# Two graph products by Strassen's scheme: three of their seven half-size products split once more

## The chip, the cores and the metric

The kernel runs on one core of one Trainium2 chip. The metric is the device time of one execution in microseconds (us). The runs of the kernel before took 618.68, 618.24 and 617.34; their median is 618.24.

## The reference

The inputs are x of shape (16, 1024, 64), that is 16 graphs ("batches") of 1024 nodes with 64 channels, and one matrix adj of 1024 x 1024. Everything is float32. Layer 0 is an attention whose scores are multiplied with adj, layer 1 a diffusion convolution with the same adj in both places; each is added to its input and normalised over the 64 channels.

```python
# layer 0
Q, K, V = x @ Wq.T + bq, x @ Wk.T + bk, x @ Wv.T
score = softmax(einsum('bnc,bmc->bnm', Q, K), axis=1)
score = einsum('bnm,mc->bnc', score, adj)
x = layernorm(x + einsum('bnm,bmc->bnc', score, V))
# layer 1, with support0 = support1 = adj
x1 = einsum('ij,bjk->bik', adj, x0)
x2 = 2 * einsum('ij,bjk->bik', adj, x1) - x0
# both supports start from x0, so the second gives the same x1 and x2
out = concatenate([x0, x1, x2, x1, x2], -1) @ weight + bias
x = layernorm(x0 + out)
```

Since both supports are adj, layer 1 with the residual comes down to x0 Wa + adj (x0 Wb) + adj (adj (x0 Wc)) with three folded 64x64 weights. The kernel computes it as two products with adj, one inside the other: Z = x0 Wb + adj (x0 Wc), and then x0 Wa + bias + adj Z. In layer 0, adj V is computed as adj x, since the value weight can be applied later. So the kernel has three products of a 1024x1024 matrix with a 1024x1024 matrix (1024 nodes by 16 batches of 64 channels).

## The kernel before

The 16 batches are worked on as 8 pairs, so a pair fills 128 columns; the 1024 nodes are 8 blocks of 128. `xs` holds x by pairs and blocks, `xT` its transposed form, `GY` the rows of x0 Wc (and, at the end, the output), `aT` the transposed adj.

**The products.** `product` computes one 1024x1024 product by Strassen's scheme in Winograd's form: seven products p1 to p7 of 512x512 quarters. The left factors are quarters of adj or the sums S1 to S4 (`left_sum`, lines 216 to 222; S3 overwrites a quarter of `aT`), the right factors are quarters of the other matrix or the sums T1 to T4 (`sums`, lines 247 to 253). Each sum is one VectorE instruction of 128 x 2048. One `step(name, g)` issues half of one of the seven products: two block rows of the result, each four matmuls of 128x512 into one PSUM bank (line 284), and then one read of the 128x1024 PSUM tile by VectorE or ScalarE (lines 300 to 304), which adds it to the place of the result. Chains of products add up in PSUM: p1, p6, p7 and p4 run on in one tile ("a"), p5 and p3 in another ("b"), p2 alone ("c"), and between two members of a chain the partial sum is read and added to another quarter of the result. So a sum that belongs to two quarters is made once.

**Order of the work.** The tiles are under a manual schedule: each engine executes its instructions in the order of the program text, and the framework adds the semaphore waits, for single tile regions. The stages are: loads, transposes and projections (to 29 us in the profile), the first product adj x (to about 125 us), the attention in 64 steps (8 pairs x 8 blocks, to 410 us), the second product (to about 502 us) and the third (to 609 us). In the attention, each step issues the scores of the step after next (line 323), the running minimum on VectorE (line 330), the exponentials on ScalarE (line 337) and the weighted sums (line 360). When a pair is done, `take`, `norm_1`, `norm_2`, `transposed` and `weigh` normalise it, transpose it and apply the folded weights, spread over the steps of the next pair. `weigh` (lines 396 to 410) leaves x0 Wc in `GY`, x0 Wa + bias in `xT` and x0 Wb in `xs`. For the last pair all this falls into the first part of the second product, between its matmuls.

The second product starts with p2 and writes its result to `Z`, which takes over the memory of `U` (the result of the first, adj x); its first read of each quarter adds x0 Wb from `xs`. The third starts from x0 Wa + bias in `xT` and writes to `GY`. `leave` (line 525 on) normalises what is finished: square on ScalarE, row sum on VectorE (line 192 or 179), the inverse root either on GpSimd (line 185) or on ScalarE and VectorE (lines 194 and 195), the scaling (line 531) on GpSimd or VectorE, and the output DMA from the SP queue. The end of the third product is cut into block rows, so that four such chains follow one another.

[...] the kernel uses them as three tiles `ps` and one tile `acc` of two banks each.

Of the kernel before, what the change touches and what calls it, by code (L numbers as in the profile page):

```python
# [9 lines left out]
FP = mybir.dt.float32  # L10
# [8 lines left out]
def gnn_kernel(  # L19
# [85 lines left out]
    def transposed(p):  # L105

        pt = ps_tile("pt")
        for k in range(K8):
            nc.tensor.transpose(pt[:, ts(k, P)], xs[:, p, k, :], ident)  # L109
        nc.scalar.activation(xT[:, p], pt, AF.Copy)  # L110
# [89 lines left out]

    att = ctx.enter_context(tc.tile_pool(name="att", bufs=1))
# [11 lines left out]

    def left_sum(S, n):
        if n == 1:
            nc.vector.tensor_add(S[1], aT[:, low, right], aT[:, high, right])
        elif n == 2:
            nc.vector.tensor_sub(S[2], S[1], aT[:, low, left])
        elif n == 3:
            nc.vector.tensor_sub(aT[:, low, right], aT[:, low, left], aT[:, low, right])  # L220
        else:
            nc.vector.tensor_sub(S[4], aT[:, high, left], S[2])

    def by_pair(t):

        return t.rearrange("p k (q f) -> p q k f", q=NP)

    def product(S, src, res, plus=None, acc_group=0):

        pairs, blocks = (slice(0, NP // 2), slice(NP // 2, NP)), (low, high)
        T, open_, seen = {}, {}, set()

        def src_q(j, c):
            return src[:, pairs[c], blocks[j]]

        def by_pair4(t):
            return t.rearrange("p k (q f) -> p q k f", q=NP // 2)  # L240

        def sums(n):
            if n == 1:
                T[1] = quarter_tile("r", "T", 1)
            t = by_pair4(S[1] if n == 3 else T[1])
            if n == 1:
                nc.vector.tensor_sub(t, src_q(0, 1), src_q(0, 0))
            elif n == 2:
                nc.vector.tensor_sub(t, src_q(1, 1), t)
            elif n == 3:  # L250
                nc.vector.tensor_sub(t, src_q(1, 1), src_q(0, 1))
            else:
                nc.vector.tensor_sub(t, src_q(1, 0), t)  # L253

        def quarter(j, c):
            return lambda k: src[:, pairs[c], j * HB + k]

        def of(t):
            return lambda k: t()[:, k]


        table = {
            "p2": (lambda k, i: aT[:, HB + k, ts(i, P)], quarter(1, 0), "c", (0, 0)),
            "p1": (lambda k, i: aT[:, k, ts(i, P)], quarter(0, 0), "a", (0, 0)),
            "p5": (lambda k, i: S[1][:, k, ts(i, P)], of(lambda: T[1]), "b", (1, 1)),
            "p3": (lambda k, i: S[4][:, k, ts(i, P)], quarter(1, 1), "b", (0, 1)),
            "p6": (lambda k, i: S[2][:, k, ts(i, P)], of(lambda: T[1]), "a", (0, 1)),
            "p7": (lambda k, i: aT[:, k, ts(HB + i, P)], of(lambda: S[1]), "a", (1, 1)),
            "p4": (lambda k, i: aT[:, HB + k, ts(HB + i, P)], of(lambda: T[1]), "a", (1, 0)),
        }  # L270
        first_of = {"p2": True, "p1": True, "p5": True}

        def step(name, g, rows=(0, 1)):
            left_of, right_of, chain, (qi, qc) = table[name]
            start = name in first_of
            if start and rows[0] == 0:
                if chain == "a" and g == acc_group:
                    open_[chain, g] = pacc.tile([P, N], FP, tag="acc", name="acc")
                else:
                    open_[chain, g] = ps_tile(name)  # L280
            pt = open_[chain, g]
            for i in rows:
                for k in range(HB):
                    nc.tensor.matmul(  # L284
                        pt[:, ts(i, H)], left_of(k, 2 * g + i), right_of(k),
                        start=(start and k == 0), stop=(k == HB - 1), skip_group_check=not start,
                    )
            got = pt.rearrange("p (i q f) -> p q i f", i=2, q=NP // 2)[
                :, :, rows[0] : rows[-1] + 1
            ]  # L290
            b0 = qi * HB + 2 * g + rows[0]

            def at(t):
                return t[:, pairs[qc], b0 : b0 + len(rows)]

            mark = (qi, qc, g, rows[0]) if len(rows) == 1 else (qi, qc, g)
            known = any(m in seen for m in (mark, mark[:3]))
            seen.add(mark)
            if known:
                nc.vector.tensor_add(at(res), got, at(res))  # L300
            elif plus is None:
                nc.scalar.activation(at(res), got, AF.Copy)  # L302
            else:
                nc.vector.tensor_add(at(res), got, at(plus))  # L304

        return step, sums
# [64 lines left out]
    def norm_1(p):  # L371
        po = ps_tile("po")
# [17 lines left out]
    def weigh(p, c):  # L390

        pw = ps_tile("pw").rearrange("p (b f) -> p b f", b=2)
# [10 lines left out]
        def at(t):  # L403
# [7 lines left out]
            xs[:, p, blocks].rearrange("p k (b c) -> p k b c", b=2), to[:, 1], AF.Copy  # L411
        )

    S = left_tiles()
    for n in (1, 2, 4, 3):
        left_sum(S, n)
    step, sums = product(S, xs, by_pair(U), acc_group=1)
    sums(1)
# [4 lines left out]
    for name in ("p2", "p1", "p5"):  # L423
        step(name, 0)
        step(name, 1)
    sums(2)
    sums(3)
    step("p3", 0)
    step("p6", 0)
    step("p6", 1)  # L430
    sums(4)
    step("p7", 0)
    step("p7", 1)
    step("p3", 1)
    step("p4", 0)
    for i in range(2):
        step("p4", 1, (i,))
        scores(i)
        for j in range(2):
            exponentials(i, j)  # L440
# [6 lines left out]

    last = len(steps) - 1
    for n, (p, m) in enumerate(steps):
        if n + 2 <= last:  # L450
            scores(n + 2)
            exponentials(n + 2, 0)
# [18 lines left out]

    def blocked(t):
        return t.rearrange("p q (k f) -> p q k f", k=K8)

    p = NP - 1
    Z = big.tile([P, K8, BC], FP, tag="uz", name="Z")
    root = const.tile([P, 1], FP, tag="root", name="root")
    nc.scalar.activation(root, eps, AF.Sqrt)
    S = left_tiles()
    step, sums = product(S, blocked(GY), by_pair(Z), xs)  # L480
    weigh(p - 1, 3)
    step("p2", 0, (0,))
    norm_1(p)
    norm_2(p, last=True)
    step("p2", 0, (1,))
    left_sum(S, 1)
    step("p2", 1)
    transposed(p)
    step("p1", 0, (0,))
    weigh(p, 0)  # L490
    weigh(p, 1)
    step("p1", 0, (1,))
    weigh(p, 2)
    weigh(p, 3)
    sums(1)
    step("p1", 1)
    left_sum(S, 2)
    left_sum(S, 4)
    step("p5", 0)
    left_sum(S, 3)  # L500
    step("p5", 1)
    sums(2)
    sums(3)
    step("p3", 0)
    step("p6", 0)
    step("p6", 1)
    sums(4)
    step("p7", 0)
    step("p7", 1)
    nc.vector.tensor_add(S[1], S[2], aT[:, low, left])  # L510
    step("p4", 0)
    step("p4", 1)
    step("p3", 1)

    R = GY.rearrange("p q n -> p (q n)").rearrange("p (k f) -> p k f", k=K8)

    def leave(i, c, g, skip=0, blocks=2):

        first_block = i * HB + 2 * g + skip
        r = R[:, first_block : first_block + blocks, ts(c, H)].rearrange(  # L520
            "p i (b c) -> p i b c", c=C
        )
        nb = B // 2
        sq = att.tile([P, blocks, nb, C], FP, tag="rT", name="sq2")
        nc.scalar.activation(sq, r, AF.Square)  # L525
        rows = sq.rearrange("p i b c -> p (i b) c")
        if blocks == 1:
            engine, rstd = nc.vector, inverse_root_2(rows, nb)
        else:
            engine, rstd = nc.gpsimd, inverse_root(row_sums(rows))  # L530
        engine.tensor_tensor(  # L531
            r, r, rstd.rearrange("p (i b) c -> p i b c", i=blocks), ALU.mult
        )
        for n in range(blocks):
            nc.sync.dma_start(out[ts(first_block + n, P), ts(c, nb)], r[:, n])

    step, sums = product(S, by_pair(Z), by_pair(R), blocked(xT))
    step("p2", 0)
    sums(1)
    step("p2", 1)  # L540
    for g in range(2):
        step("p1", g)
        leave(0, 0, g)
    step("p5", 0)
    step("p5", 1)
    sums(2)
    sums(3)
    step("p3", 0)
    step("p6", 0)
    leave(0, 1, 0)  # L550
    step("p6", 1)
    sums(4)
    for g in range(2):
        step("p7", g)
        leave(1, 1, g)
    step("p4", 0)
    leave(1, 0, 0)
    for i in range(2):
        for name, q in (("p4", (1, 0)), ("p3", (0, 1))):
            step(name, 1, (i,))  # L560
            leave(*q, 1, i, 1)
# [40 lines left out]
```

## Time and profile before

| | before |
|---|---|
| median of the runs | 618.24 us |
| the profiled execution, its own time | 617.97 us |
| its span | 616.0 us |
| busy: TensorE / VectorE / ScalarE / GpSimd | 605.6 / 337.1 / 226.0 / 78.4 us |
| TensorE busy in the second and third product (410 to 609 us) | 198.9 of 199.0 us |
| VectorE busy there | 81.9 us |
| mean granted TensorE clock | 0.997 of full speed |
| longest row of waits that ended TensorE's idle time | 1.5 us in all, for the first transposes |

The profile shows one execution. Lines of the form "start, length, engine, line, operation, out<-in, shape" are instructions in order of time; what stands in brackets is the idle time before an instruction and what ended it. A float32 matmul shows as two records, each with its own weight load (PEld). The length of a VectorE instruction reaches to the moment its result is written; the next one may start some 0.08 us before that.

### The profile page before, as it was taken

The page shows a single profiled execution, that of the slowest core. Times are in us where ns is not written, and L with a number is a line of the kernel's source. Part 1 is how long each engine was busy: PE and PEld are TensorE (multiplying, and loading weights), DVE is VectorE, ACT ScalarE, POOL GpSimd, SP SyncE. Part 2 cuts the span into 40 slices and gives each one's busy share as a digit, 9 for nine tenths or more (in the row PEclk, how much of TensorE's full clock was granted, in tenths as well). Part 3 has the DMA queues.
Part 4 walks back from the last instruction along what each step waited for, and adds up shares of the span by engine and source line. Part 5 has one row for each costly group of instructions (what it writes and reads, how often), then busy time and mean ns, then how long its engine had stood idle before and what let it go on. Part 6 is the DMA issues. An engine that isn't in the chain of part 4 may idle for free. (4 is left out here: it accounts for less than half of the span.)

```text
span 616.0 us, 5816 instructions
## 1 busy us (share of the span) xinstructions
PE 605.6 (98%) x2270; PEld 264.4 (43%) x2270; DVE 337.1 (55%) x560; ACT 226.0 (37%) x379; POOL 78.4 (13%) x40
## 2 busy tenths in 40 slices
PE   8999999999999999999999999999999999999995
PEld 7544444433334344443434434344444444444442
DVE  1696212067677767677776767735462333224535
ACT  4210110156666666676666667651100000000012
POOL 0000004400030300203030020300000000150372
PEclk9999999999999999999999999999999999999998
DMA  8700000000000000000000000000000000010012
GB/s 302 263 0 1 0 1 36 33 0 1 1 1 0 2 1 1 1 1 1 1 0 2 0 2 1 0 1 0 1 0 1 0 0 0 1 69 0 34 70 102
DMA packets 6763, 14.30 MB, mean 23 GB/s; under 512 B 2000, under 2 KB 2000, under 8 KB 6736
## 3 DMA queue, kind: packets, MB, share of 16 engines
q1 hardware_dynamic: 6416, 13.90, 6.1%
q8 instruction: 18, 0.29, 0.2%
q10 hardware_dynamic: 320, 0.03, 0.0%
q14 instruction: 9, 0.07, 0.0%
HBM read 9.73 MB, written 4.19 MB: 23 GB/s over the span
## 5 line engine op out<-in xcount | busy, mean ns | idle before, releaser
L330 DVE TENSOR_SCALAR_CACHE_REDUCE e<-sc 128x1024 f32<-128x1024 f32 x128 | 151.6, 1222 | 68.1 <-PE sc L323 68.1
L337 ACT ACTIVATE e<-e,nm 128x1024 f32<-128x1024 f32 x128 | 146.2, 1143 | 74.6 <-DVE e L330 74.5
L323 PE MATMUL sc<-xT,GY 64*128 64x512 f32 x512 | 128.1, 615 | 0.5 <-DVE e L330 0.5
L360 PE MATMUL acc<-e,us 128*64 128x512 f32 x512 | 124.0, 605 | 0.3 <-DVE us L348 0.3
L185 POOL TENSOR_TENSOR rstd<-var,expo 128x16 f32<-128x16 f32 x13 | 37.7, 2901 | 421.5 <-DVE var L180 421.5
L323 PEld LDWEIGHTS sc<-xT,GY 64*128 64x128 f32 x512 | 44.6, 186 | 73.5 <-issue 49.9
L525 ACT ACTIVATE sq<-GY 128x1024 f32<-128x1024 f32 (+1 forms) x10 | 8.9, 886 | 159.6 <-DVE GY L300 149.9
L284 PE MATMUL p<-T,S 128*128 128x512 f32 x144 | 62.8, 592 | 0.0
L360 PEld LDWEIGHTS acc<-e,us 128*64 128x64 f32 x512 | 31.0, 136 | 71.0 <-issue 62.9
L284 PEld LDWEIGHTS p<-T,S 128*128 128x128 f32 x144 | 27.4, 190 | 34.4 <-issue 34.4
L302 ACT ACTIVATE U<-p 128x1024 f32<-128x1024 f32 x6 | 6.1, 1024 | 76.3 <-PE p L284 76.3
L396 PEld LDWEIGHTS pw<-raw,xT 64*128 64x128 f32 x256 | 21.8, 187 | 17.3 <-issue 7.3
L444 POOL TENSOR_TENSOR xs<-xs,mu 128x1024 f32<-128x1024 f32 x8 | 15.0, 1901 | 102.8 <-DVE T L253 92.0
L396 PE MATMUL pw<-raw,xT 64*128 64x192 f32 x256 | 27.1, 332 | 0.0
L407 DVE TENSOR_TENSOR xT<-pw,raw 128x256 f32<-128x256 f32 x32 | 13.6, 425 | 21.3 <-ACT GY L406 21.3
L337 ACT ACTIVATION_READ_ACCUMULATOR e<-e,nm 128x1 f32 x128 | 24.0, 188 | 0.0
L110 ACT ACTIVATE xT<-pt 128x1024 f32<-128x1024 f32 x16 | 16.2, 1014 | 17.2 <-PE pt L109 17.2
L284 PE MATMUL acc<-T,aT 128*128 128x512 f32 x48 | 21.4, 594 | 0.0
L284 PE MATMUL p<-GY,aT 128*128 128x512 f32 x48 | 21.3, 596 | 0.0
L284 PE MATMUL p<-T,aT 128*128 128x512 f32 x48 | 21.3, 592 | 0.0
L284 PE MATMUL acc<-T,S 128*128 128x512 f32 x48 | 21.1, 592 | 0.0
L284 PE MATMUL p<-S,aT 128*128 128x512 f32 x48 | 21.1, 592 | 0.0
(116 smaller groups left out, 585.4 us busy)
## 6 DMA issues: line engine op xcount, KB each, us to landing
aT<-in_adjT_dram SPq DMA_DIRECT2D x8, 512.0 KB, 11.3
out_dram<-GY SPq DMA_DIRECT2D x16, 256.0 KB, 2.2
xs<-in_x_dram SPq DMA_DIRECT2D x7, 512.0 KB, 6.4
aT<-in_adjT_dram SPq DMA_DIRECT2D x1, 1024.0 KB, 5.2
xs<-in_x_dram SPq DMA_DIRECT2D x2, 256.0 KB, 3.0
w1s<-in_w_dram SPq DMA_DIRECT2D x2, 80.0 KB, 10.0
wq<-in_wqT_dram ACTq DMA_DIRECT2D x2, 16.0 KB, 3.3
wk<-in_wkT_dram SPq DMA_DIRECT2D x2, 16.0 KB, 3.1
```

Source lines behind the costliest of these rows:

```text
L110: nc.scalar.activation(xT[:, p], pt, AF.Copy)
L185: nc.gpsimd.tensor_tensor(rstd, var, expo[:, 0:g], ALU.pow)
L284: nc.tensor.matmul(pt[:, ts(i, H)], left_of(k, 2 * g + i), right_of(k), start=(start and k == 0), stop=(k == HB - 1), skip_group_check=not ...
L302: nc.scalar.activation(at(res), got, AF.Copy)
L323: nc.tensor.matmul(sc[j][:, ts(h, H)], GY[s, p, ts(m, P)], xT[s, p, ts(h, H)], start=True, stop=True,)
L330: nc.vector.tensor_scalar(E[n][:, j], sc[j], -1.0, None, op0=ALU.mult, op1=ALU.min, accum_out=NM[n][:, j : j + 1],)
L337: nc.scalar.activation(E[n][:, j], E[n][:, j], AF.Exp, bias=NM[n][:, j : j + 1], scale=-1.0, accum_out=SM[n][:, j : j + 1],)
L360: nc.tensor.matmul(ACC[p][j * C : (j + 1) * C, ts(h, H)], us[:, j], es[:, j, ts(h, H)], start=(m == 0), stop=(m == K8 - 1),)
L396: nc.tensor.matmul(pw[:, j, ts(k, 3 * C)], xT[s, p, ts(2 * c + k, P)], raw[s, 0:3].rearrange("p w c -> p (w c)"), start=True, stop=True,)
L407: nc.vector.tensor_tensor(at(xT), to[:, 0], raw[:, 4:5, None].to_broadcast([P, 2, 2, C]), ALU.add)
L444: nc.gpsimd.tensor_tensor(rows_of(p), rows_of(p), mu[:, p, :, None].to_broadcast([P, G, C]), ALU.subtract)
L525: nc.scalar.activation(sq, r, AF.Square)
```

## The change

The second and third product are issued by a new class `Product`. It differs from `product` in these points.

- Every left and right sum is four instructions of 128 x 512 (one for each block of rows) instead of one of 128 x 2048. This holds for the first product as well.
- A list `line` holds pieces of VectorE work that wait to be issued. `later` appends to it, `fill(n)` issues the next n, `need(names)` issues from it until no piece of these names is left. `step` issues its matmuls, then its reads, then `fill(fills)`.
- In the second and third product the half-size products 2, 3 and 4 are each split again by the same scheme: `halves` gives the eight sums of 256x256 quarters (each one VectorE instruction of 128 x 512, kept in the memory of `xs`), and `part` issues one of the seven small products, four matmuls of 128x256 into one bank and one VectorE read of 128 x 512. Parts 1, 6, 7 and 4 share one bank, 5 and 3 another, 2 has its own.
- Products 3 and 4 no longer add up in the PSUM chains; so the PSUM tiles of 5 and of 7 are read into two quarters each (`twice`).
- `weigh` leaves x0 Wb in `U`, the place of adj x, a pair at a time after that pair's attention; the second product adds to it there, and the third reads it. `Z` is gone.
- The second product starts with product 1 and the tile of the attention's accumulator; the order is 1, 2, 5, 3, 6, 7, 4 in both. The first eight small sums are issued in the last eight steps of the attention.
- `leave` works on two blocks by four or eight batches; its first instruction, the square, is issued at once and the rest is put at the head of `line`.

The diff, cut to its core:

```diff
     def left_sum(S, n):
-        if n == 1:
-            nc.vector.tensor_add(S[1], aT[:, low, right], aT[:, high, right])
-        elif n == 2:
-            nc.vector.tensor_sub(S[2], S[1], aT[:, low, left])
-        elif n == 3:
-            nc.vector.tensor_sub(aT[:, low, right], aT[:, low, left], aT[:, low, right])
-        else:
-            nc.vector.tensor_sub(S[4], aT[:, high, left], S[2])
+        to, a, b, op = {
+            1: (S[1], aT[:, low, right], aT[:, high, right], ALU.add),
+            2: (S[2], S[1], aT[:, low, left], ALU.subtract),
+            3: (aT[:, low, right], aT[:, low, left], aT[:, low, right], ALU.subtract),
+            4: (S[4], aT[:, high, left], S[2], ALU.subtract),
+        }[n]
+        return [
+            lambda k=k: nc.vector.tensor_tensor(to[:, k], a[:, k], b[:, k], op)
+            for k in range(HB)
+        ]
...
+    line = []
+    def later(name, pieces):
+        line.extend((name, piece) for piece in pieces)
+    def fill(n):
+        for _ in range(min(n, len(line))):
+            line.pop(0)[1]()
+    def need(*names):
+        while any(name in names for name, _ in line):
+            fill(1)
...
+        def targets(self, name):
+            return {
+                1: [(0, 0)], 2: [(0, 0)], 3: [(0, 1)], 4: [(1, 0)], 6: [(0, 1)],
+                5: [(1, 1)] + [(0, 1)] * (3 in self.twice),
+                7: [(1, 1)] + [(1, 0)] * (4 in self.twice),
+            }[name]
...
+        def step(self, name, g, fills=0, rows=(0, 1)):
+            self.matmuls(name, g, rows)
+            self.read(name, g, rows)
+            fill(fills)
...
+        def halves(self, name, room):
+            a, b = self.factors(name)
+            W = H // 2
+            la = [[a[:, 2 * j : 2 * j + 2, ts(i, W)] for j in range(2)] for i in range(2)]
+            rb = [[b[:, 2 * c : 2 * c + 2, 2 * j : 2 * j + 2] for c in range(2)] for j in range(2)]
+            s, t, raw_t = {}, {}, {}
+            for n in range(1, 5):
+                s[n] = room[:, ts(n - 1, H)].rearrange("p (k i) -> p k i", k=2)
+                t[n] = by_pair(room[:, ts(n + 3, H)].rearrange("p (k f) -> p k f", k=2))
+            self.sub = {
+                1: (la[0][0], rb[0][0]), 2: (la[0][1], rb[1][0]), 3: (s[4], rb[1][1]),
+                4: (la[1][1], t[4]), 5: (s[1], t[1]), 6: (s[2], t[2]), 7: (s[3], t[3]),
+            }
+            sub, add = nc.vector.tensor_sub, nc.vector.tensor_add
+            lefts = [
+                lambda: add(s[1], la[1][0], la[1][1]), lambda: sub(s[2], s[1], la[0][0]),
+                lambda: sub(s[3], la[0][0], la[1][0]), lambda: sub(s[4], la[0][1], s[2]),
             ]
+            rights = [
+                lambda: sub(t[1], rb[0][1], rb[0][0]), lambda: sub(t[2], rb[1][1], t[1]),
+                lambda: sub(t[3], rb[1][1], rb[0][1]), lambda: sub(t[4], rb[1][0], t[2]),
+            ]
+            return lefts, rights
...
+        def part(self, name, q, two_tiles):
+            a, b = self.sub[q]
+            tile_, bank = {1: (0, 0), 6: (0, 0), 7: (0, 0), 4: (0, 0), 2: (1, 0)}.get(q, (1, 1))
+            pt = two_tiles[tile_][:, ts(bank, H)]
+            start = q in (1, 2, 5)
+            W = H // 2
+            for i in range(2):
+                for k in range(2):
+                    nc.tensor.matmul(
+                        pt[:, ts(i, W)], a[:, k, ts(i, P)], b[:, :, k],
+                        start=(start and i == k == 0), stop=(k == 1), skip_group_check=True,
+                    )
+            (i, c), = self.targets(name)
+            di, dc = {1: (0, 0), 2: (0, 0), 6: (0, 1), 3: (0, 1), 7: (1, 1), 5: (1, 1), 4: (1, 0)}[q]
+            self.take(pt, i * HB + 2 * di, 2, c * NP // 2 + 2 * dc, 2)
+    PARTS = (1, 2, 6, 5, 7, 3, 4)
...
-            xs[:, p, blocks].rearrange("p k (b c) -> p k b c", b=2), to[:, 1], AF.Copy
+            U[:, blocks, ts(p, P)].rearrange("p k (b c) -> p k b c", b=2), to[:, 1], AF.Copy
...
+        if p == NP - 1:
+            if m == 0:
+                later("half", [f for both in zip(*hop_1.halves(2, room[0])) for f in both])
+            fill(1)
...
+    need("half")
     S = left_tiles()
+    hop_1.S = S
     weigh(p - 1, 3)
+    h = [pacc.tile([P, N], FP, tag="acc", name="h0")] + [ps_tile(f"h{n}") for n in (1, 2, 3)]
+    hop_1.tiles = [h[0], h[2], h[1], h[3]]
+    for n in (1, 2, 4):
+        later(f"S{n}", left_sum(S, n))
+    hop_1.matmuls(1, 0, (0,))
+    norm_1(p, h[1])
     norm_2(p, last=True)
+    hop_1.matmuls(1, 0, (1,))
+    hop_1.read(1, 0)
+    two = (h[2], h[3])
+    hop_1.part(2, 1, two)
+    fill(1)
+    hop_1.part(2, 2, two)
+    fill(1)
+    transposed(p, h[1])
+    hop_1.part(2, 6, two)
+    fill(1)
+    hop_1.part(2, 5, two)
+    fill(1)
+    weigh(p, 0, h[1])
+    hop_1.part(2, 7, two)
+    hop_1.part(2, 3, two)
+    weigh(p, 1, h[1])
+    hop_1.part(2, 4, two)
+    weigh(p, 2, h[3])
+    weigh(p, 3, h[1])
+    need("S1")
+    line[:0] = [("T1", f) for f in hop_1.right_sum(1)]
+    hop_1.step(1, 1, 7)
+    two = (h[1], h[3])
+    SUB_DONE = {2: (0, 0), 7: (1, 1), 3: (0, 1), 4: (1, 0)}
+    def turns(product, room, after_5, after_6):
+        S = product.S
+        need("S1", "T1")
+        lefts, rights = product.halves(3, room[0])
+        later("half", [f for both in zip(lefts, rights) for f in both])
+        for g in range(2):
+            product.step(5, g, 6)
+        need("half")
+        later("T2", product.right_sum(2))
+        later("T3", product.right_sum(3))
+        for q in PARTS:
+            product.part(3, q, two)
+            fill(1)
+        need("S2", "T2")
+        if after_5:
+            later("S3", left_sum(S, 3))
+        lefts, rights = product.halves(4, room[1])
+        later("half", lefts)
+        for g in range(2):
+            product.step(6, g, 5)
+            after_6(g)
+        need("S3", "T3")
+        later("T4", product.right_sum(4))
+        later("half", rights)
+        for g in range(2):
+            product.step(7, g, 4 if after_5 else 5)
+            if not after_5:
+                leave(1, 1, g)
+        need("half")
+    turns(hop_1, room[::-1], True, lambda g: None)
+    later("S1", [
+        lambda k=k: nc.vector.tensor_add(S[1][:, k], S[2][:, k], aT[:, k, left])
+        for k in range(HB)
+    ])
+    for q in PARTS:
+        hop_1.part(4, q, two)
+        fill(1)
+    need("S1")
...
+        def rest():
+            engine = nc.gpsimd
+            if half is not None and i:
+                rstd = inverse_root_2(rows, 2 * nb)
+                if (g, half) == (1, 0):
+                    engine = nc.vector
+            else:
+                rstd = inverse_root(row_sums(rows, 2 * nb), 2 * nb)
+            engine.tensor_tensor(
+                r, r, rstd.rearrange("p (i b) c -> p i b c", i=2), ALU.mult
+            )
+            for n in range(2):
+                nc.sync.dma_start(out[ts(first_block + n, P), b0 : b0 + nb], r[:, n])
+        line.insert(0, ("leave", rest))
+    hop_2 = Product(S, by_pair(U), by_pair(R), hop_1.tiles, xT.rearrange("p q (k f) -> p q k f", k=K8), (2, 3, 4))
+    later("T1", hop_2.right_sum(1))
+    lefts, rights = hop_2.halves(2, room[0])
+    later("half", [f for both in zip(lefts, rights) for f in both])
     for g in range(2):
+        hop_2.step(1, g, 6)
+    need("half")
+    for q in PARTS:
+        hop_2.part(2, q, two)
+        fill(1)
+        if q in SUB_DONE:
+            leave(0, 0, *SUB_DONE[q])
+    turns(hop_2, room[::-1], False, lambda g: leave(0, 1, g))
+    for q in PARTS:
+        hop_2.part(4, q, two)
+        fill(1)
+        if q in SUB_DONE:
+            leave(1, 0, *SUB_DONE[q])
+    need("leave")
```

## The prediction

> **What bounds the kernel now.** I read the page's busy shares first, then the busy time by stage, then the chain of waits, then the timeline where the change acts. In the stage answer the columns are window, length, then busy time of PE, weight loads (PEld), DVE, ACT and POOL, the granted clock and the DMA.
>
> ```profile
> span 616.0 us, 5816 instructions
> PE 605.6 (98%) x2270; PEld 264.4 (43%) x2270; DVE 337.1 (55%) x560; ACT 226.0 (37%) x379; POOL 78.4 (13%) x40
> ```
>
> ```profile
> 410.00:502.00 92.00, 92.00 (x262) 43.12 (x259) 40.84 (x32) 7.95 (x16) 0.00 (x0) 1.00 0.00 0
> 502.00:609.00 107.00, 106.87 (x250) 46.96 (x248) 41.01 (x42) 9.14 (x12) 29.07 (x12) 1.00 0.09 35
> 609.00:616.00 7.00, 0.00 (x0) 0.00 (x0) 2.67 (x5) 0.93 (x2) 0.00 (x0) 0.77 0.20 75
> ```
>
> The second and third product run from 410 to 609 us with TensorE never idle and VectorE busy 82 of 199 us. So TensorE work is the bound there, and VectorE has room, but only on average. The chain of waits (start, length, engine) gives the rate of each kind of matmul:
>
> ```profile
> 410.34 3.63 PE p L284 x8
> 413.98 1.78 PE po L375 x16
> ...
> 478.40 6.87 PE acc L284 x16
> 485.27 6.87 PE p L284 x16
> ```
>
> One f32 matmul is two records. A half-product of 8 matmuls 128x512 takes 6.87, so a record of 512 columns takes 0.4293 us; one of 128 columns takes 1.78/16 = 0.111. The timeline gives VectorE's prices:
>
> ```profile
> 471.57 1.22 DVE L300 TENSOR_TENSOR Z<-acc,Z 128x1024 f32<-128x1024 f32 x1 [5.64 <-PE acc L284]
> 492.17 1.22 DVE L300 TENSOR_TENSOR Z<-p,Z 128x1024 f32<-128x1024 f32 x1 [5.64 <-PE p L284]
> 493.31 2.28 DVE L510 TENSOR_TENSOR S<-S,aT 128x2048 f32<-128x2048 f32 x1
> 597.65 1.22 DVE L179 TENSOR_REDUCE var<-sq 128x16 f32<-128x1024 f32 x1 [1.25 <-ACT sq L525]
> 598.99 0.69 DVE L304 TENSOR_TENSOR GY<-p,xT 128x512 f32<-128x512 f32 x1
> 608.79 0.69 DVE L531 TENSOR_TENSOR GY<-GY,rstd 128x512 f32<-128x512 f32 x1
> 609.40 0.68 DVE L300 TENSOR_TENSOR GY<-p,GY 128x512 f32<-128x512 f32 x1
> ```
>
> A read of 1024 PSUM columns costs 1.14 when another instruction follows (493.31 - 492.17), 1.22 when somebody waits for it; 512 columns cost 0.61 (609.40 - 608.79) and 0.69; a row sum with its scaling 1.34 (598.99 - 597.65). PE's end to DVE's start is 0.04 (471.53 by the chain, to 471.57), DVE to PE 0.06:
>
> ```profile
> 404.49 0.29 DVE L348 TENSOR_TENSOR us<-U,ri 128x128 f32<-128x128 f32 x1
> 404.84 0.20 PEld L360 LDWEIGHTS acc<-e,us 128*64 128x64 f32 x4 [0.55 <-DVE us L348]
> ```
>
> [...] So cutting one 2048-column sum (2.28) into four makes it 4 x 0.61 = 2.44. [...] before, TensorE always found its bank read. [...] Here it was granted 0.77 over the last, idle 7 us, which fits half speed from 3.8 us on.
>
> **TensorE work removed.** Each of the products 2, 3 and 4 was 16 matmuls of 512 columns, 13.74. It becomes 7 parts of 4 matmuls of 256 columns. The trace has no such matmul at 128 rows: between the rows of 128 and 512 columns a record comes to 0.2173[...]; I take 0.2165. A part is 8 records = 1.73, seven are 12.12. Saved: 1.62 x 6 = 9.7 (9.4 to 9.9). Weight loads (0.19 busy) fit under it, as they even did at 0.111.
>
> **VectorE work added, and where it stands.** Per hop, 12 full reads for 14 (5 and 7 are read into two places), but 21 part reads and 24 half sums more. On average it still fits. But VectorE works in order, and `step` issues matmuls, their reads, and then `fill`: the sums of the last half-product therefore stand behind its reads, in front of the first part's read. Parts 1, 6, 7, 4 share one bank, so part 6 may not start before part 1 is read, and only part 2 (1.73) lies between. From the end of the big product TensorE has work for 3.46; VectorE needs 0.04 + reads + sums + 0.69, and 0.06 more to PE. Ahead of part 1's read stand:
>
> - hop 1, product 3: 2 reads, 7 sums (`fill(6)` and one left to `need`): 0.04+2.28+4.27+0.69+0.06 = 7.34, a wait of 3.88 (0.73 of it ahead of part 2, whose bank the second read empties);
> - hop 1, product 4: 2 reads, 4 sums, one straight on its predecessor (+0.12): 5.63, wait 2.17;
> - hop 2, product 2: 1 read, 6 sums: 5.59, wait 2.13;
> - hop 2, product 3: 2 reads, 3 sums: 4.90, wait 1.44;
> - hop 2, product 4: 2 reads, a row sum of the output's normalisation 1.34, 4 sums (+0.12): 6.97, wait 3.51.
>
> Together 13.1. Hop 1's product 2 has its sums made during the last pair of attention, in VectorE's idle 0.75 to 2.0 us per step; I cost them at nothing (without that cover 8 x 0.61 = 4.9). Three more waits: in hop 1 the first right sum T1 now stands behind the read of product 1's second half, and product 5 needs its first piece: 0.04+1.14+0.69+0.06 = 1.93. In hop 2 product 5 starts in the bank of the last part: 0.04+0.69+0.06 = 0.79. Hop 1's first matmul uses the attention accumulator's tile, which ACT still copies until 410.56 while PE was free at 410.34: 0.28. That makes 16.1. Ten resumptions each show a first weight load, about 0.1: 1.0. Behind the waiting matmuls stands all of TensorE's queue; nobody else can fill it.
>
> In the other half-products VectorE needs 4.2 to 6.5 of 6.87, no backlog; the first product's sums in pieces cost about 1 us more, beside 13.7 us matmul stretches. Attention's x0 Wb is one ACT copy to another tile: nothing. POOL and the SP queue get more, smaller outputs in hop 2, in time except at the end.
>
> **The end.** Before: matmuls end at 608.87, the last scaling at 612.95, 4.08 later. After, from the last part: its read starts 0.21 late, the pending group's row sum and root (to 1.88), then square, row sum, root, reciprocal and scaling of the last, ending at 4.58: +0.5. Two output DMAs instead of one: 0 to 0.8, I take 0.4.
>
> **Sum.** -9.7 + 16.1 + 1.0 + 0.9 = +8.3 on the profiled execution's 617.97 (span 616.0 and 2 us around it): 626.3. The runs' median, 618.24, is 0.27 above that execution, so 626.5.
>
> **Rivals.**
> - *TensorE's work decides, faster.* If VectorE's sums do not hold the matmuls up, only 0.3 + 0.9 stays: 618.24 - 9.7 + 1.2 = 609.7. For it: TensorE is 98% busy, VectorE 55%. Against: the order on VectorE. It takes over where the waits and resumptions fall below 8.8, that is, if the 24 sums counted above cost under 0.27 each rather than 0.61, or did not stand there. 0.12.
> - *The waits also cost the clock.* Two idle stretches, 3.2 and 3.5 us, come near the 3.8 after which the clock fell here. Each fall would run some 3.4 us at half speed, 1.7 lost: up to 630. 0.12.
> - *256 columns are too short.* If a record costs 0.240 since its weight load shows, the saving shrinks by 336 x 0.0235 = 7.9: 634.4. Against: the 128-column rows. 0.06.
> - *The forecast*, 626.5: 0.70. Its own range: sums at 0.73 if each waits for its predecessor, 24 x 0.12 = +2.9; resumptions 0 to 0.2, -1 to +1; records -0.2 to +0.3; DMA -0.4 to +0.4; and waits shortened where the sums are not needed at once: 622 to 630.
>
> **Range and chances.** 621 to 631 leaves out the first rival, the third and a little of the forecast. 0.2%, 1.2 us, is about what a measurement of this kernel can tell from no change. Faster 0.12, within 0.02, slower 0.86.
>
> **What would show it.** Matmuls of 256 columns at 0.217 per record; PE idle of 2 to 4 us ahead of part 6 in five of six sub-products, ended by DVE's read of part 1; 1.9 us ahead of hop 1's product 5, ended by T; VectorE full in those gaps; no such gap in hop 1's product 2; attention unchanged. If PE stays at 98% busy, the forecast is wrong and the first rival right.

## The result and the profile after

| | before | after |
|---|---|---|
| median of the runs | 618.31 us (617.34 to 618.68) | 634.28 us (632.16 to 635.29) |
| ratio, 95% interval | | 1.0256 (1.0226 to 1.0286) |
| the profiled execution, its own time | 617.97 us | 633.71 us |
| its span | 616.0 us | 631.9 us |
| mean granted TensorE clock | 0.997 | 0.986 |

The median of the kernel before at the start of this document, 618.24, is that of three of these four runs. The change costs 16 us; 8.3 were forecast, and the time lies 3.3 above the range. The first lines of the page after, its totals, and the rows of TensorE and of its clock over 40 slices of 15.8 us:

```profile
span 631.9 us, 6267 instructions
...
PE 606.1 (96%) x2414; PEld 297.0 (47%) x2414; DVE 391.5 (62%) x706; ACT 226.2 (36%) x381; POOL 84.2 (13%) x47
...
PE   9999999999999999999999999999879989899974
...
PEclk9999999999999999999999999999989999899988
```

TensorE is busy as long as before (605.6), though six of its products now take seven eighths of their matmul work. So some matmuls took longer, and the row of the granted clock says where to look: at the four 8s in the last eleven slices. Attention, to 410 us, is as it was. What TensorE waited for (total, times, longest):

```profile
PE h L375 <- DVE GY L309: 5.9, 3, 3.5
PE h L375 <- DVE U L309: 5.7, 3, 2.8
PE h L322 <- DVE T L276: 2.0, 1, 2.0
```

All three rows were foretold: VectorE's read of PSUM (L309), and the first right sum T (L276). L322 stands for the matmuls of half products, L375 for those of parts; "hop 1" and "hop 2" are the second and the third product. The timeline has the waits in their places; the first number is the start, the second the length of the row, the bracket the idle time ahead of it:

```profile
445.40 13.97 PE L322 MATMUL h<-T,S 128*128 128x512 f32 x32 [2.01 <-DVE T L276]
...
461.82 2.00 PE L375 MATMUL h<-GY,S 128*128 128x256 f32 x8 [0.72 <-DVE U L309]
466.63 7.13 PE L375 MATMUL h<-xs 128*128 128x256 f32 x24 [2.81 <-DVE U L309]
...
510.26 5.45 PE L375 MATMUL h<-xs 128*128 128x256 f32 x24 [2.12 <-DVE U L309]
...
538.42 7.13 PE L375 MATMUL h<-xs 128*128 128x256 f32 x24 [2.07 <-DVE GY L309]
...
568.69 5.45 PE L375 MATMUL h<-xs 128*128 128x256 f32 x24 [0.41 <-DVE GY L309]
...
611.97 8.27 PE L375 MATMUL h<-xs 128*128 128x256 f32 x24 [3.45 <-DVE GY L309]
```

What VectorE did ahead of part 6 at 466.63: the two reads of product 5, seven small sums (L356 to L361, the first and the last shown), and only then the read of part 1, 0.06 us behind whose end part 6 starts:

```profile
459.41 2.35 DVE L309 TENSOR_TENSOR U<-h,U 128x1024 f32<-128x1024 f32 x2 [0.71 <-PE h L322]
461.68 0.68 DVE L360 TENSOR_TENSOR xs<-GY 128x512 f32<-128x512 f32 x1
...
465.29 0.68 DVE L361 TENSOR_TENSOR xs<-GY,xs 128x512 f32<-128x512 f32 x1
465.89 0.68 DVE L309 TENSOR_TENSOR U<-h,U 128x512 f32<-128x512 f32 x1
```

The five rows of 24 records are the same work (parts 6, 5 and 7). Two take 5.45 us, two 7.13 and one 8.27. The lost 1.68 + 1.68 + 2.82 = 6.2 us are no waits: the matmuls themselves ran slower. Why, the busy times by stretch show (window, length, busy time of PE, PEld, DVE, ACT, POOL, then the granted clock):

```profile
464.00:468.00 4.00, 1.37 (x5) 1.20 (x6) 4.00 (x8) 0.00 (x0) 0.00 (x0) 0.94 0.00 0
468.00:472.00 4.00, 4.00 (x13) 3.22 (x12) 1.66 (x3) 0.00 (x0) 0.00 (x0) 0.63 0.02 4
...
608.00:612.00 4.00, 0.55 (x4) 0.14 (x2) 3.93 (x8) 1.06 (x1) 3.13 (x1) 0.86 0.35 131
612.00:616.00 4.00, 4.00 (x10) 3.19 (x11) 2.92 (x4) 0.63 (x1) 3.81 (x3) 0.50 0.25 95
```

Behind a stretch with TensorE mostly idle and VectorE full (0.55 and 3.93 of 4 us at 608), the clock is at half speed (0.50 over the next 4 us). By the trace's own clock records it fell to half three times before the end: 467.52 to 470.93, 539.20 to 542.61 (3.41 us each) and 610.88 to 617.71 (6.83 us). These are the "falls" from here on.

Where the 15.9 us of span went, by the first and last matmuls of the stages in both traces: +0.5 ahead of the second product (410.27, then 410.80), +5.9 in the second product (102.3, then 108.2), +8.6 in the third (95.7, then 104.3), +0.85 from the last matmul's start to the end.

### The profile page after: what moved, and what is told of

It is laid out like the page before. It is cut to its first block, busy times and chain, and to the rows that moved or that the text cites. A ratio compares the mean times of both kernels' runs of the same rounds, so it can differ in the third digit from the quotient of the medians.

```text
span 631.9 us, 6267 instructions
## 1 busy us (share of the span) xinstructions
PE 606.1 (96%) x2414; PEld 297.0 (47%) x2414; DVE 391.5 (62%) x706; ACT 226.2 (36%) x381; POOL 84.2 (13%) x47
## 4 chain that ended last, share of the span: by engine, by line
PE 90%; DVE 7%; DMA 1%; issue 1%; ACT 1%; POOLq 0%; POOL 0%; ACTq 0%
PE h L322 32%; PE sc L400 20%; PE acc L437 19%; PE h L375 10%; PE pw L473 3%; PE po L452 2%; PE pt L109 2%; PE pg L131 2%; DVE U L309 1%; DVE GY L313 1%; DMA xs<-in_x_dram 1%; DVE xs L360 1%; DVE xs L361 1%; DVE xs L357 1%; PE h L473 1%
## 5 line engine op out<-in xcount | busy, mean ns | idle before, releaser
L185 POOL TENSOR_TENSOR rstd<-var,expo 128x16 f32<-128x16 f32 (+1 forms) x15 | 40.0, 2664 | 433.6 <-DVE var L180 433.5
L322 PE MATMUL h<-T,S 128*128 128x512 f32 x192 | 83.6, 593 | 2.8 <-DVE T L276 2.0
L309 DVE TENSOR_TENSOR U<-h,U 128x512 f32<-128x512 f32 (+1 forms) x39 | 36.1, 935 | 63.6 <-PE h L322 52.6
L322 PEld LDWEIGHTS h<-T,S 128*128 128x128 f32 x192 | 36.4, 190 | 48.0 <-issue 46.3
L375 PE MATMUL h<-xs 128*128 128x256 f32 x144 | 39.1, 436 | 10.9 <-DVE GY L309 5.9
L322 PE MATMUL h<-S,aT 128*128 128x512 f32 x96 | 41.7, 593 | 0.0
L375 PEld LDWEIGHTS h<-xs 128*128 128x128 f32 x144 | 31.1, 220 | 18.4 <-DVE GY L309 7.1
L309 DVE TENSOR_TENSOR GY<-h,GY 128x512 f32<-128x512 f32 (+1 forms) x25 | 19.3, 772 | 24.8 <-PE h L322 13.1
L322 PEld LDWEIGHTS h<-S,aT 128*128 128x128 f32 x96 | 18.3, 190 | 22.9 <-issue 22.7
L322 PE MATMUL h<-xs,aT 128*128 128x512 f32 x64 | 27.6, 592 | 0.0
L473 PEld LDWEIGHTS pw<-raw,xT 64*128 64x128 f32 x224 | 19.2, 187 | 15.8 <-issue 5.8
```

The costliest lines, as they stand in the source:

```text
L185: nc.gpsimd.tensor_tensor(rstd, var, expo[:, 0:g], ALU.pow)
L309: nc.vector.tensor_add(at(self.res), got, at(self.res))
L322: nc.tensor.matmul(pt[:, ts(i, H)], a[:, k, ts(2 * g + i, P)], b[:, :, k], start=(start and k == 0), stop=(k == HB - 1), skip_group_check= ...
L375: nc.tensor.matmul(pt[:, ts(i, W)], a[:, k, ts(i, P)], b[:, :, k], start=(start and i == k == 0), stop=(k == 1), skip_group_check=True,)
L473: nc.tensor.matmul(pw[:, j, ts(k, 3 * C)], xT[s, p, ts(2 * c + k, P)], raw[s, 0:3].rearrange("p w c -> p (w c)"), start=True, stop=True,)
```

## The experiments

The theory: VectorE's order makes the waits; the longer waits also make the clock fall, and this second part is what the forecast left out. Rival 1: the excess over the forecast is dearer small matmuls or contention, and the clock only goes along. Rival 2: VectorE has too much to do in these stages, whatever the order. Each run's own "before" on its chip was 617.9 to 618.3.

### Gaps put into the kernel before: long ones

`hold` names p6 0, p6 1 and p7 1 of the second product:

```diff
+            if (name, g) in hold:
+                spare = att.tile([P, N], FP, tag="rT", name="spare")
+                nc.vector.tensor_add(spare, pt, aT[:, 0])
+                for _ in range(12):
+                    nc.vector.tensor_sub(spare[:, 0:H], aT[:, 0, left], aT[:, 1, left])
             if known:
```

> The kernel before, with work added on VectorE alone: behind three half products of the first hop one more read of an accumulator and 12 sums of 512 columns into a tile that nothing reads, ahead of the read that TensorE's next matmul waits for, so that TensorE gets three gaps of about 2.9 us each. No matmul is added or split. Theory (gaps of this length lower the clock): 8.7 us of gaps, and 1.7 us for each fall that they bring: 627 with none, 628.7 to 632 with one to three, and the granted clock below 0.99. Rival 1 (the clock is not the gaps' doing): 627 us and the clock at 0.996.

633.49 us (632.90 to 634.64), ratio 1.0251 (1.0236 to 1.0267). Its timeline:

```profile
482.88 8.82 PE L284 MATMUL acc<-S,aT 128*128 128x512 f32 x16 [4.30 <-DVE Z L305]
493.86 7.13 PE L284 MATMUL p<-S,aT 128*128 128x512 f32 x16 [2.15 <-DVE Z L309]
500.83 7.03 PE L284 MATMUL acc<-T,aT 128*128 128x512 f32 x16
512.15 9.54 PE L284 MATMUL p<-T,aT 128*128 128x512 f32 x16 [4.29 <-DVE Z L305]
```

The gaps came out longer than planned, 10.7 us in all for 8.7, so the time lies above the 628.7 to 632 that the theory named. A half product of 16 records takes 7.03 (7.13 behind a wait); behind the two gaps of 4.3 it takes 8.82 and 9.54, behind the one of 2.15 not. The clock records have a fall of 3.41 us at 482.90 and one of 6.83 at 510.21. The span is 15.8 above that of before: 10.7 of gaps, 1.7 and 2.4 for the slower records in these two rows, 0.2 of a later start, and some 0.8 for three resumptions (0.28 each in the next run). So waits lowered the clock here with no matmul split and no part added. Rival 1, with a clock at 0.996, is out: the clock was 0.990, and gaps of 10.7 us with their resumptions alone would have made about 629.6.

### Gaps put into the kernel before: short ones

The same edit with `range(7)`, at p6 0 and p7 1 of both products.

> The kernel before with VectorE work added as in the run with long gaps, but 7 sums instead of 12 and at four places (two of each hop), so that TensorE gets four gaps of about 1.3 us instead of two of 4.3 and one of 2.2. In the runs so far the clock fell behind every window of 3.41 us in which TensorE was busy 42% or less and behind none at 46% or more; a gap of 1.3 us leaves at least 62%. Theory: no fall, the time is that of the kernel before and the gaps alone, 618.1 + 5 = 623, the clock at 0.996. Rival (any wait of TensorE costs more than its length): 625 or more.

626.23 us (625.09 to 627.00), ratio 1.0132 (1.0115 to 1.0149). The clock had no fall before the end, as the theory says, but the time is 3 us above what I wrote. Its trace accounts for that without the clock: five gaps of 0.67, 0.67, 0.67, 1.19 and 1.13 us, 4.3 in all; the two products are longer by 1.9 and 3.8, so each gap costs 0.28 more than it shows; from the last matmul to the end it is 2.0 more, since the sums at p7 1 of the third product also hold up the output's normalisation; and the first matmul of the second product came 0.8 later, with 2.7 instead of 1.5 us of waits for the input at the start. The expectation forgot the normalisation. The rival's number was met, and in part by what it says: 1.4 us are what the five gaps cost beyond their length. That cost is a resumption at each gap, though, not the clock.

### Matmuls that fill the waits, first try

In `part`, behind the matmuls of part 2 and ahead of its read, with `idle` 6, 5, 4, 1 and 8 in the order of the five products:

```diff
+            for _ in range(idle):
+                nc.tensor.matmul(
+                    two_tiles[0][:, H : H + W], a[:, 0, ts(0, P)], b[:, :, 0],
+                    start=True, stop=True, skip_group_check=True,
+                )
```

> The changed kernel with 24 matmuls of 128x256 added, whose results nothing reads, behind part 2 of five products: 6, 5, 4, 1 and 8 of them, in the waits ahead of part 6, each set shorter than its wait. VectorE's queue and the waits' ends stay where they are. Theory (the clock fell because TensorE stood idle): the clock stays near 0.996 and the 6.3 us go, about 628 us, though 24 matmuls more are issued. Rival 1 (the extra time is dearer matmuls or contention, and the falls only go along with it): 634 us or a little more.

641.96 us (640.56 to 645.84), ratio 1.0389 (1.0371 to 1.0406). It tested nothing of what it was made for: its waits now stand at the filler's own line (5.9 and 4.9 us in all), since the filler writes the second bank of the tile whose first bank VectorE is still to read. The fillers ran behind the waits: 24 x 0.43 = 10.3 us more, and a fourth fall at 445.73, 1.7, make 12.0 of the 12.1 that its profiled execution lies above that of the changed kernel.

### Matmuls that fill the waits, second try

The loop stands where it stood, ahead of the read of part 2 (the expectation below takes this place for new). What changes is the tile that it writes, which is now part 2's own:

```diff
-                    two_tiles[0][:, H : H + W], a[:, 0, ts(0, P)], b[:, :, 0],
+                    two_tiles[1][:, H : H + W], a[:, 0, ts(0, P)], b[:, :, 0],
```

> The filler run mended: the same 24 extra matmuls of 128x256, whose results nothing reads, now stand ahead of part 2's read and write the other half of part 2's own tile, so that they wait for nothing that is late. A matmul of this kind is two records of 0.216 us, so the sets take 2.6, 2.2, 1.7, 0.4 and 3.4 us, within 0.05 us of their waits or shorter. Theory (the falls of the clock come from idle TensorE): waits' ends stay, TensorE is busy through them, none of the three falls is left unless the wait for T at 445 us brings one: 628 (629.7 with that one). Rival 1 (the 6 us over the forecast are not the falls): 634 or more, whatever the clock.

629.91 us (628.87 to 631.08), ratio 1.0195 (1.0178 to 1.0211), for 629.7 expected with one fall left; the profiled execution is the one of 631.08. Two of the filled waits in its timeline (the rows of L380 are fillers):

```profile
508.75 2.32 PE L380 MATMUL h<-T,aT 128*128 128x256 f32 x10
511.04 5.45 PE L375 MATMUL h<-xs 128*128 128x256 f32 x24
...
607.44 3.62 PE L380 MATMUL h<-T,aT 128*128 128x256 f32 x16
611.05 1.99 PE L375 MATMUL h<-xs 128*128 128x256 f32 x8
613.88 3.72 PE L375 MATMUL h<-xs 128*128 128x256 f32 x16 [0.84 <-DVE GY L309]
```

TensorE starts part 6 when VectorE lets it, as before, but has been busy until then, and the kernel with 24 matmuls more is 4.4 us faster. Behind the filled waits all parts run at full speed (5.45 us, where a fall made it 7.13 and 8.27). One fall is left, at 446.53, behind the wait for T of 2.00 us, which was not filled; the same wait (2.01) brought none in the changed kernel's profile. In the third product alone, from first to last matmul, the time went from 104.3 to 100.9: minus 1.68 and 2.82 of clock, plus 0.84 of a new wait, and 0.25 that I did not follow up. So the falls cost time themselves and do not merely go along with something else: VectorE's queue is the same, TensorE is kept busy, and where the falls are gone their time is gone. Rival 1 (634 or more) is out.

### Part 5 ahead of part 6

```diff
-    PARTS = (1, 2, 6, 5, 7, 3, 4)
+    PARTS = (1, 2, 5, 6, 7, 3, 4)
```

> The changed kernel with part 5 ahead of part 6, so that the second small product of every filled product starts one part (1.73 us) later against VectorE's queue. Theory (queue order makes the waits, and the longer ones also cost the clock): the four waits ahead of part 6 at full length shrink by 1.73 us each and the shortest by its 0.7, 7.6 us in all, and most of the three falls of the clock (6.3 us) go with them: about 620.5 us, and 617 to 623 with none to one fall left. Rival 1 (the extra time over the forecast is not the clock but dearer small matmuls): only the 7.6 us go, about 626.7. Rival 2 (VectorE's amount of work is the limit, not its order): the waits come back at other parts, 630 or more.

649.37 us (645.68 to 649.62), ratio 1.0492 (1.0463 to 1.0521). The theory's number and rival 1's were wrong; rival 2's, 630 or more with the waits at other parts, was met. The timeline (VectorE and TensorE around one product 4) shows what the new wait is for:

```profile
512.13 0.69 DVE L309 TENSOR_TENSOR U<-h,U 128x512 f32<-128x512 f32 x1
512.73 0.68 DVE L637 TENSOR_TENSOR S<-S,aT 128x512 f32<-128x512 f32 x1
513.33 0.69 DVE L309 TENSOR_TENSOR U<-h,U 128x512 f32<-128x512 f32 x1
513.93 0.68 DVE L637 TENSOR_TENSOR S<-S,aT 128x512 f32<-128x512 f32 x1
514.07 6.47 PE L375 MATMUL h<-xs 128*128 128x256 f32 x16 [3.33 <-DVE U L309]
...
521.32 1.99 PE L375 MATMUL h<-xs 128*128 128x256 f32 x8 [0.78 <-DVE U L309]
```

Part 5 starts 0.05 us after the end of the second L309, the read of part 2, which stands one sum behind the read of part 1. Its bank is its own; its tile of two banks is shared with part 2, and the wait is for the tile. The waits here are not for regions within a tile, as the part on the order of work has it. And part 7 now follows part 6 directly in one bank: 0.78 of bare read each time. The waits grow from 15.4 to 26.6 us, and the longer ones bring falls of 3.41, 6.83, 3.41 and 6.83 us. The order 1, 2, 6, 5, 7, 3, 4 of the change alternates between the two tiles and is the better one. This run alone leaves rival 2 open; the last two runs below, with the same sums and reads on VectorE, rule it out.

### The read behind the sums, and part 2 in another bank

```diff
         def step(self, name, g, fills=0, rows=(0, 1)):
             self.matmuls(name, g, rows)
-            self.read(name, g, rows)
             fill(fills)
+            self.read(name, g, rows)
...
-            tile_, bank = {1: (0, 0), 6: (0, 0), 7: (0, 0), 4: (0, 0), 2: (1, 0)}.get(q, (1, 1))
+            tile_, bank = {1: (0, 0), 6: (0, 0), 7: (0, 0), 4: (0, 0), 2: (0, 1)}.get(q, (1, 1))
```

Besides, the numbers of sums per half product are shifted, hop 2's small sums of product 2 go ahead of its T1, and product 5 of hop 2 begins with its second half.

> The changed kernel's arithmetic with VectorE's queue put in another order: each step issues the small sums ahead of the read instead of behind it, and the sums are spread over earlier half products, so that they lie where VectorE waits for TensorE anyway; part 2 goes to another bank; hop 2's small sums stand ahead of T1; product 5 of hop 2 computes its second half first. Theory (order makes the waits): nearly all of the 15.4 us of waits and all falls of the clock go: 610 to 612.5 us, below the kernel before. Rival 2 (VectorE's amount of work in these stages is the limit): waits of 8 us or more stay, 620 or more. Rival 1 (dearer matmuls rather than the clock): 616 to 618.

627.08 us (626.47 to 627.71), ratio 1.0145 (1.0130 to 1.0160). This lies between the two kernels and far from the theory's 610 to 612.5, for the reason that the run before has just shown. One of its products:

```profile
502.81 1.89 PE L375 MATMUL h<-T,aT 128*128 128x256 f32 x8
506.01 1.99 PE L375 MATMUL h<-T,aT 128*128 128x256 f32 x8 [1.32 <-DVE U L309]
508.79 5.45 PE L375 MATMUL h<-xs 128*128 128x256 f32 x24 [0.78 <-DVE U L309]
```

Part 2 in the tile of part 1 waits for part 1's read (1.32), and part 6 for part 2's (0.78). That leaves 12.8 us of waits, 12.5 of them in eleven pieces, the longest 2.4. Yet the clock of the profiled execution had no fall before the end (0.997): 2.6 us less of waits than in the changed kernel, in shorter pieces, and 7.2 us less of time. The expectation's numbers for rival 2 were met, but not by VectorE's load: the next run moves one bank.

### Part 2 put back

```diff
-            tile_, bank = {1: (0, 0), 6: (0, 0), 7: (0, 0), 4: (0, 0), 2: (0, 1)}.get(q, (1, 1))
+            tile_, bank = {1: (0, 0), 6: (0, 0), 7: (0, 0), 4: (0, 0), 2: (1, 0)}.get(q, (1, 1))
```

> The read-behind kernel with one thing put back: part 2 in the tile of parts 3 and 5, as in the changed kernel, instead of in the tile of parts 1 and 6. The trace of the read-behind kernel shows the waits at part 2 (for the read of part 1) and at part 6 (for the read of part 2) though the banks differ, so a tile makes the wait. Theory (order and tiles make the waits, VectorE's amount of work doesn't): the ten waits of 0.8 to 1.5 us, 10.2 us in all, go, but for up to 0.7 at part 2 of each product 3; the one of 2.4 at 424 us goes too if the tile made it; no fall of the clock before the end: 612.5 to 616, below the kernel before. Rival 2 (VectorE's amount of work is the limit): the waits gather ahead of part 6 again, 8 us or more, 622 or more.

612.26 us (611.78 to 613.26), ratio 0.9911 (0.9896 to 0.9926): 0.9% faster than the kernel before, clear of the interval, and just below the range I gave. In the second and third product 0.27, 0.72 and 0.72 us of waits are left.

### The swap alone

Is it the swap in `step`, or the spreading of the sums? The changed kernel with nothing else edited:

```diff
         def step(self, name, g, fills=0, rows=(0, 1)):
             self.matmuls(name, g, rows)
-            self.read(name, g, rows)
             fill(fills)
+            self.read(name, g, rows)
```

> The changed kernel with two lines of step swapped and nothing else: the small sums of a half product are issued ahead of its read instead of behind it. They then run while TensorE still computes the half product, when VectorE was idle, and only the reads are queued between the end of a product and part 1. Theory (the order of VectorE's queue makes the waits, these make the falls): of the waits only 0.7 at part 2 of each product 3 and up to 1 in all elsewhere are left, no fall before the end, 612 to 614.5, as the read-behind kernel with part 2 put back (612.3). Rival 2 (the spreading of the sums over earlier half products was needed, there is too much work for one place): 618 or more, with waits ahead of part 6 of 2 us and more left in hop 2, where row sums stand in the queue too.

613.10 us (612.95 to 613.62), ratio 0.9919 (0.9905 to 0.9932). Two lines swapped take 21 us off the changed kernel. By the two profiled spans it is 20.7: 12.9 of waits (15.4, then 2.5), 6.2 of falls, and 1.6 for six resumptions less at 0.27 each. Its page and its timeline around the start of product 3 in hop 1:

```profile
PE 597.0 (98%) x2414; PEld 291.2 (48%) x2414; DVE 391.3 (64%) x706; ACT 226.2 (37%) x381; POOL 84.3 (14%) x47
...
PEclk9999999999999999999999999999999999999998
```

```profile
455.56 0.68 DVE L357 TENSOR_TENSOR xs<-S,xs 128x512 f32<-128x512 f32 x1
456.88 1.89 PE L375 MATMUL h<-GY,S 128*128 128x256 f32 x8
457.08 2.36 DVE L309 TENSOR_TENSOR U<-h,U 128x1024 f32<-128x1024 f32 x2 [0.83 <-PE h L322]
459.35 0.68 DVE L361 TENSOR_TENSOR xs<-GY,xs 128x512 f32<-128x512 f32 x1
459.49 1.99 PE L375 MATMUL h<-GY,S 128*128 128x256 f32 x8 [0.72 <-DVE U L309]
459.95 0.68 DVE L309 TENSOR_TENSOR U<-h,U 128x512 f32<-128x512 f32 x1
...
461.32 4.91 PE L375 MATMUL h<-xs 128*128 128x256 f32 x22
```

Of the small sums (L356 to L361) one is left between the two reads of product 5 (L309, x2) and part 1's read; the others ran before 456.25, while TensorE was still at product 5. VectorE does the same work as in the changed kernel (391.3 us busy; there 391.5) and even has 0.83 us to spare there. Rival 2 is out. What the spreading of the sums adds on top (612.26) can't be told from nothing: the intervals of the two ratios overlap.

## Why the prediction was wrong, point by point

The sign was right and the time was not. In the forecast's own steps:

- **TensorE work removed: right.** The starts of its records lie 0.2159 us apart (mean of 280 with no wait or fall between) for 0.2165, which was my estimate, a little under the 0.2173 between the rows of 128 and 512 columns. A record of 512 columns takes 0.4292 in the trace of before, so one of 256 costs half of that and 0.0013 more. The saving is 9.9, at the upper end of its 9.4 to 9.9; the rival of the short columns is out.
- **The waits: right, each in its place.** Forecast ahead of part 6 (with the 0.73 at part 2) 3.88, 2.17, 2.13, 1.44 and 3.51; measured 2.81 + 0.72 = 3.53, 2.12, 2.07, 0.41 + 0.77 = 1.18, and 3.45. T1 2.01 for 1.93, hop 2's product 5 0.78 for 0.79, the accumulator's tile 0.27 for 0.28. In all 15.4 for 16.1.
- **Resumptions: more than twice too small.** Taken at 0.1 each. The first record behind a wait does take 0.10 longer than the others (0.32 to the next start for 0.216). But the last one ahead of a wait also counts as busy for 0.38, where without a wait the next starts after 0.216. So a wait costs 0.27 beyond the idle time, 2.4 us in nine waits; the run with short gaps had 0.28 each.
- **The end: right.** The last scaling ends 4.42 us after the last matmul by the timeline (before 4.08), 0.3 more for 0.5; the output's transfer adds 0.7 for 0.4.
- **The step that failed is the one that is not in the sum: the clock.** The forecast read from the tail of the kernel before that the clock falls 3.8 us into an idle stretch (by its clock records at 612.77, 3.90 behind the last matmul), saw that its waits of 3.2 and 3.5 us "come near the 3.8", and charged nothing; the falls became a rival with 0.12, 1.7 us each, up to 630. So the falls were seen, but left out of the sum, and too small in the rival. It cost 6.2 us in the profiled execution. Two things were wrong. The idle time needed was read too long: the falls came behind waits of 2.81, 2.07 and 3.45. And a fall was counted too short: two ran for 3.41 us and cost 1.68 each, as the rival had it, but the last ran for 6.83 and cost 2.82. The rest of the miss of 7.4 is 1.4 of resumptions and small terms of both signs.

The sum with this term, on the profiled execution: 617.97 - 9.9 + 15.4 + 2.4 + 6.2 + 1.3 (start 0.26 beyond the accumulator's tile; 1.07 from the end of the last matmul on) = 633.4 for 633.71. The last 0.3 stays open.

No fixed idle time fits the falls: in the changed kernel they came 3.70, 2.85 and 2.36 us after TensorE had gone idle. What fits is the time between them. In each trace with more than one fall, all lie a whole number of 3.41 us apart (in the changed kernel 467.52, 539.20 and 610.88, twice 71.68 = 21 x 3.413). So I cut the second and third product of the ten traces into windows of this length, counted from the falls (the one in the idle end of the kernel where there was no other), and took TensorE's busy share of each that began at full speed, with the modelled ends of its matmuls. The lowest shares were:

| TensorE busy in a window | windows | fall right behind it |
|---|---|---|
| 0.00 to 0.31 (without the ends of the kernels) | 8 | 8 |
| 0.39 to 0.42 | 6 | 6 |
| 0.46 to 0.50 | 5 | 0 |

The line was found in these traces, so runs that came after it count most: it was written down, in the expectation for the short gaps, before four of the ten kernels ran (short gaps, second filler, part 2 put back, swap alone). In them one window had 41%, with a fall behind it; all others had 65% or more, without one.

The ends of the falls sort the same way: nine falls lasted one window (3.41 us), and in all nine TensorE was busy for 99% or more of it; five lasted two (6.83 us), and in these its share in the first was 43 to 82% (43 in the run with long gaps, 68 in the changed kernel).

So the place of a wait mattered as much as its length. In the changed kernel the one of 2.07 at 538 lay in one window whole (39% busy) and brought a fall; those at 445 (2.01) and 510 (2.12) lay across two, with 48% busy in the lower one, and left the clock alone. The wait for T brought a fall in both filler runs; in the second, its 2.00 us lay in one window (41%). That may also be why the changed kernel's runs differ by 3 us and those of before by 1.3; that is not shown, since the falls of one execution of each kernel alone are on record.

The rival "TensorE's work decides", 609.7, failed here as the forecast said, by the order on VectorE. With the order mended it is nearly true: 613.1 with 2.5 us of waits and their resumptions left.

## What to carry to other kernels

VectorE, busy for 62% of the span, held up TensorE, which had been busy for 98% before: ask what stands in its queue between an event and the instruction that others wait for, and put the work that nobody waits for ahead of it, where the engine idles. Price a TensorE wait twice, by its length and by the clock: in these runs some waits of 2.0 us and more were followed by a fall that cost 1.7 us on top, or 2.4 to 2.9 where it ran for 6.83 us. Waits of up to 1.6 us cost no clock in these runs, but 0.27 each beyond their length. Ask of every wait whether it is for a bank or for the whole tile that holds it.

## What the runs showed that I had not expected

- In these traces the clock fell behind every window of 3.41 us in which TensorE was busy 42% or less and behind none at 46% or more; it rose again behind those in which TensorE was busy for 99% or more, and not behind those at 43 to 82%. A fall of 3.41 us cost 1.7 us, one of 6.83 cost 2.4 (the long gaps), 2.8 (the changed kernel) or 2.9 (part 5 ahead). Where between 42 and 46% the line lies, and whether it moves with the kind of matmul, was not tried.
- A PSUM tile of two banks is one thing to the waits here, whatever the part on the order of work says of tile regions: matmuls into one bank waited for VectorE's read of the other (3.33 us instead of 2.12 in the run with part 5 ahead).
- Each wait of TensorE cost 0.27 us more than the idle time that the profile shows in the changed kernel, and 0.28 in the run with short gaps.
- Filling idle TensorE with useless matmuls paid here: 24 of them took 4.4 us off the changed kernel (634.28, then 629.91), though not waiting at all took 21 off (613.10).
